# Four-layer graph network: single heads project values first, the adjacency is turned by DMA, wider ANDs, mask products summed in PSUM

## The chip, the cores and the metric

The kernel runs on one core of a Trainium2 chip. A core has four computing engines with queues of their own: TensorE (PE, matrix products into the PSUM banks), VectorE (DVE), ScalarE (ACT) and GpSimd (POOL), and a fifth, SyncE (SP), which here only issues DMAs; in the changed kernel POOL issues some too. The metric is the device time of one execution in microseconds (us), as the median of several runs.

## The reference

Sixteen graphs of 1024 nodes and 128 features go through four attention layers. In each one the layer's output is added to its input and normalized over the features:

```python
x = _layernorm(x + _L0_gnn_ref(x, adj, ...))   # typed attention
x = _layernorm(x + _L1_gnn_ref(x, adj, ...))   # single head, slope 0.01
x = _layernorm(x + _L2_gnn_ref(x, adj, ...))   # 8 heads, then a single head, with graph norms
x = _layernorm(x + _L3_gnn_ref(x, adj, ...))   # single head, slope 0.2
```

A single head computes `h = x @ W`, two scores per node `s = h @ a_src`, `t = h @ a_dst`, the weights `softmax(where(adj > 0, leaky_relu(s[:, None] + t[None, :]), -inf))`, and `weights @ h`. The eight-head part does this for eight heads of 16 features, with the features viewed as `(heads, nodes, 16)`. The typed layer 0 chooses one of eight bilinear scores by the entry of the adjacency. `adj` is an int32 array of 0 and 1, 4 MB a graph, with ones on the diagonal.

## The kernel before

The input of each graph is 1024 x 1024 adjacency entries and 1024 x 128 features; nodes lie as 128 partitions by G = 8 groups. All work of the fast path is written by `graph(b)` for b = 0 to 15 (L862), not issued at once: a `Recorder` (L113) collects the operations, and `rc.run` simulates engines with a cost for each operation and fixes one order per engine for all sixteen graphs together. Among operations that can start at the same time it takes the one with the lowest due time (`wanted`: its number in the program plus shifts from a table), lets up to two later graphs start ahead (`AHEAD`), and gives operations that ACT or DVE could do (`rc.either`: copies, scalings, biases, comparisons) to the one that is free earlier, with a handicap (`LATER`). All instructions of `graph` are issued from line L424, so rows of the profile are told apart by tiles. Each engine then runs its own list strictly in order. Tiles come from shelves with a fixed number of places: `maskT` 3, `row` 26 (4 KB a partition), `half` 11, `bank` 8 (the PSUM banks).

The steps of one graph:

- **Mask.** For each of eight row blocks SP loads 512 KB of int32 (`raw`), ACT casts it to bf16 (`eb`, a `half`), PE turns it in 128 x 128 squares, and ACT writes the squares to `maskT` as fp8, with value 2. Both ACT passes keep sums (`e_sum`, `e_sq`), by which an entry other than 0 and 1 is found at the end; then the general path runs instead.
- **Layer 0 (typed).** Two score products per square (128 x 512 columns, f32) are merged by DVE's COPY_PREDICATED on `maskT`; then a leaky relu, a maximum over the graph (`graph_max`), exponentials and the sum over the values.
- **Layers 1 and 3 (`single_head`, L798).** The weight of node j on all nodes is max(a_row, ratio_j) x mask, one DVE instruction for 128 x 1024 (`weights_of`). `a_row`, the factor of the receiving node repeated on all partitions, is made by `factors`: a matmul of a widened score vector (`srcw`) with hT in two halves of 512 columns, and two ACT exponentials of it. The scaled inputs are then the stationary operand and the weights move through in two halves of 512 columns (`av`), 32 passes of PE in all; the sums are copied to SBUF (`avT`) and only then multiplied with the layer's matrix (`w_v`).
- **Layer 2, eight heads.** exp(leaky_relu(s + t)) is split into two products by the sign of s + t. `mask_sums(g)` multiplies `maskT` with the low-slope factors of all heads (three bf16 parts each, `m4`): eight matmuls of 408 columns, and a DVE reduction of the three parts. `products(h)` makes, for two groups j at a time, the sign mask `q` (a `half`, fp8, ACT or DVE), ANDs it with `maskT` (DVE, 1024 uint16) and multiplies with 102 columns of `m4`. Its row of scores `s1_row` comes by DMA through DRAM (`s1d`).
- **Layer 2, second part (`projected_head`, L830).** Here the values are projected first and are the moving operand: 8 x 8 matmuls of 129 columns with squares of the weights as the stationary operand, and no product after it.

SP's queue, in a graph of the middle: the store of a finished graph, the eight adjacency loads and the load of the features of a coming one, the store `s1d`, and eight loads of `s1_row`.

Of the kernel before, what the change touches and what calls it, by code (L numbers as in the profile page):

```python
# [15 lines left out]
U8 = mybir.dt.uint8  # L16
AF = mybir.ActivationFunctionType
# [3 lines left out]
P = 128  # L21
D = 128
# [86 lines left out]
class Op:  # L109
    __slots__ = ("ways", "way", "skip", "graph", "rank", "before", "after", "ready", "slots", "missing", "late")  # L110


class Recorder:  # L113
# [4 lines left out]
    DMA_RATE, DMA_FIXED = 370.0, 2200.0  # L118

    def __init__(self, nc, tc):  # L120
        self.nc, self.tc, self.ops, self.graph = nc, tc, [], 0
        self.access = {}
        self.rate, self.used = [0.5], collections.Counter()
# [37 lines left out]
    def cost_of(self, engine, name, args, kw, outs, ins):  # L161
# [6 lines left out]
        if engine == "tensor":  # L168
            n = self.width(o)
            left = kw.get("lhsT", args[1] if len(args) > 1 else None)  # L170
            left = left.ap if isinstance(left, View) else left
            apart = abs(list(left.ap)[-1][0]) > 4
            if name == "transpose":
                return 112.0 if f32 else 62.0 if apart else 45.0, 165.0
            if f32:
                return 2 * max(n * 2 / 2.4, 238.0 if apart else 112.0), 165.0
            return max(n * 0.478 if n > 300 else n * 0.43, 45.0), 165.0
# [3 lines left out]
        if engine == "gpsimd":  # L181
            return 300.0, 50.0
# [32 lines left out]
    def either(self, *ways, skip=None):  # L215
# [4 lines left out]
        op.graph, op.ways, op.way, op.skip = self.graph, [], None, skip  # L220
# [39 lines left out]

    WINDOW, BUSY = 3413.0, 0.9

    def spend(self, t, work):

        while True:
            w = int(t // self.WINDOW)
            while len(self.rate) <= w:
                self.rate.append(1.0 if self.used[len(self.rate) - 1] > self.BUSY * self.WINDOW else 0.5)
            room = (w + 1) * self.WINDOW - t
            took = min(room, work / self.rate[w])  # L270
            self.used[w] += took
            t += took
            work -= took * self.rate[w]
            if work <= 1e-6:
                return t

    def run(self, rank, window, later):
# [62 lines left out]
        def admit(i):  # L340
            for way in ops[i].ways:
                pools[way[0]].append((i, way, ranks[i] + (later.get(way[0], 0) if len(ops[i].ways) > 1 else 0)))
# [25 lines left out]
        while len(order) < n:  # L368
# [38 lines left out]
            end = self.spend(t, way[4]) if way[0] == "tensor" else t + way[4]  # L407
# [28 lines left out]
def gnn_stack_kernel(ctx: ExitStack, tc: tile.TileContext, w: dict, out: bass.AP):  # L436
# [11 lines left out]
    def fast_path(stack):  # L448
# [144 lines left out]
        def row_weights(scores, name):  # L593
            src_wide = const([P, P], name + "_srcw")
            nc.vector.tensor_copy(src_wide, scores[0].to_broadcast([P, P]))
            return src_wide, scores[1]

        shift = const([P, P], "shift")
        nc.vector.memset(shift, 0.0)
        nc.vector.tensor_copy(shift[:, 0 : D - 1], ident[:, 1:D])
        nc.vector.memset(shift[0:1, 0 : D - 1], -1.0)

        def without_first(wt, name):
            ps = ps_const(D)
            nc.tensor.matmul(ps, lhsT=shift, rhs=wt, start=True, stop=True)
            t = const([P, D + 1], name)
            mean = ppool.tile([P, 1], F32, tag="mean", name="mean")  # L610
            nc.vector.tensor_reduce(mean, ps, AX.X, ALU.add)
            nc.vector.tensor_scalar(mean, mean, 1.0 / D, None, ALU.mult)
            nc.vector.tensor_scalar(t[:, 0:D], ps, mean, None, ALU.subtract)
            nc.vector.tensor_copy(t[:, D : D + 1], ident[:, D - 1 : D])
            return t

        w1_r, w2b_r, w3_r = row_weights(w1_s, "l1"), row_weights(w2b_s, "l2b"), row_weights(w3_s, "l3")
        w1_v, w3_v = without_first(w1, "w1_v"), without_first(w3T, "w3_v")
        w2b_e = const([P, D + 1], "w2b_e")
        nc.vector.tensor_copy(w2b_e[:, 0:D], w2b)  # L620
        nc.vector.tensor_copy(w2b_e[:, D : D + 1], w2b_s[1])
# [19 lines left out]
        e_sum = const([P, B, G], "e_sum")  # L641
        e_sq = const([P, B, G], "e_sq")
# [19 lines left out]
        PLACES = {"maskT": 3, "row": 26, "half": 11}  # L662
# [8 lines left out]
        shelves["dram"] = Shelf("dram", [dram.tile([NH, N], F32, tag=f"s1d{k}", name=f"s1d{k}")[:, :] for k in range(2)])  # L671

# [23 lines left out]
        def copy(dst, src):  # L696
            rc.either(("scalar", "copy", (dst, src), {}), ("vector", "tensor_copy", (dst, src), {}))

        def affine(dst, src, scale, shift):
# [3 lines left out]
                ("vector", "tensor_scalar", (dst, src, scale, shift, ALU.mult, ALU.add), {}),  # L703
            )

        def scaled(dst, src, scale):
# [3 lines left out]
                ("vector", "tensor_scalar", (dst, src, scale, None, ALU.mult), {}),  # L710
            )
# [48 lines left out]
        def graph_max(v):  # L760
# [4 lines left out]
            rc.tensor.transpose(ps[0:1, :], top, ident)  # L765
            top1 = small("top1", 1, 1)
            rc.vector.tensor_reduce(top1, ps[0:1, :], AX.X, ALU.max)
            ps = bank(1)
            rc.tensor.matmul(ps, lhsT=ones[0:1, :], rhs=top1, start=True, stop=True)
            return ps  # L770

        def factors(src_wide, hT, s2, alpha, e):
# [3 lines left out]


            c2 = small("c2", P, 2)
            rc.vector.tensor_scalar(c2, coef[alpha], graph_max(s2), None, ALU.mult)
            rc.scalar.activation(e, s2, AF.Exp, bias=c2[:, 0:1])  # L780
            ratio = small("ratio", P, G)
            rc.scalar.activation(ratio, s2, AF.Exp, bias=c2[:, 1:2], scale=alpha - 1.0)
            a_row = row(N)
            for k, c in enumerate(HALVES):
                ps = bank(H, P)
                rc.tensor.matmul(ps, lhsT=src_wide, rhs=hT[:, c, :], start=True, stop=True)
                rc.scalar.activation(
                    a_row[:, k * H * P : (k + 1) * H * P], ps.rearrange("p g q -> p (g q)"), AF.Exp,
                    bias=c2[:, 1:2], scale=1.0 - alpha,
                )  # L790
# [7 lines left out]
        def single_head(x, hT, maskT, weights, wv, alpha, e, rden, finish):  # L798

            src_wide, dst = weights  # L800
            s2_ps = bank(G)
            for j in range(G):
                rc.tensor.matmul(s2_ps[:, j : j + 1], lhsT=hT[:, j, :], rhs=dst, start=True, stop=True)
            s2 = small("s2c", P, G)
            rc.vector.tensor_copy(s2, s2_ps)
            a_row, ratio = factors(src_wide, hT, s2, alpha, e)
            xe = row(G, D)
            for j in range(G):
                scaled(xe[:, j, :], x[:, j, 1 : D + 1], e[:, j : j + 1])
            av = [bank(H, P) for _ in HALVES]  # L810
            for j in range(G):
                prob = weights_of(j, a_row, ratio, maskT)
                for k in range(2):
                    rc.tensor.matmul(
                        av[k], lhsT=xe[:, j, :],
                        rhs=prob[:, k * H * P : (k + 1) * H * P], start=(j == 0), stop=(j == G - 1),
                    )
            avT = row(G, P)
            for k, c in enumerate(HALVES):
                copy(avT[:, c], av[k])  # L820
            for g0 in range(0, G, 3):
                n = min(3, G - g0)
                o = bank(n, D + 1)
                for i in range(n):
                    rc.tensor.matmul(o[:, i, :], lhsT=avT[:, g0 + i, :], rhs=wv, start=True, stop=True)
                rc.vector.reciprocal(rden[:, g0 : g0 + n].unsqueeze(2), o[:, :, D : D + 1])
                for i in range(n):
                    finish(g0 + i, o[:, i, 0:D], rden[:, g0 + i : g0 + i + 1])

        def projected_head(hT, maskT, src_wide, w_e, alpha, e, rden, finish):  # L830

            s2 = small("s2c", P, G)
            val = row(G, D + 1)
            parts = []
            for g0 in range(0, G, 3):
                n = min(3, G - g0)
                ps = bank(n, D + 1)
# [3 lines left out]
                rc.vector.tensor_copy(s2[:, g0 : g0 + n].unsqueeze(2), ps[:, :, D : D + 1])  # L841
            a_row, ratio = factors(src_wide, hT, s2, alpha, e)
# [19 lines left out]
        def graph(b):  # L862
# [4 lines left out]
            for ib in range(G):  # L867
                raw = row(N, dt=I32)
                rc.sync.dma_start(out=raw, in_=adj_b[ib])
                eb = tile_on("half", [P, N], BF16)  # L870
                rc.scalar.activation(eb, raw, AF.Identity, accum_out=e_sum[:, b, ib : ib + 1])
                ps = bank(G, P, dt=BF16)
                for j in range(G):
                    rc.tensor.transpose(ps[:, j, :], eb.rearrange("p (q g) -> p g q", g=G)[:, j, :], ident_bf)
# [224 lines left out]
            for g in range(G):  # L1099
                mask_sums(g)  # L1100
# [745 lines left out]
```

## Time and profile before

| | before |
|---|---|
| median of 3 runs | 2647.28 us (2645.2 to 2647.3) |
| the profiled execution: span | 2644.0 us, 3.3 us under the median |
| PE busy | 2531.0 us (96%) |
| DVE busy | 2386.2 us (90%) |
| ACT busy | 2014.7 us (76%) |
| POOL busy | 12.7 us |
| moved by DMA | 156.39 MB, 59 GB/s over the span |
| mean granted TensorE clock | 0.985 |

The table shows one execution. The page gives each engine's busy time, and 40 slices of the span with a digit for the tenths of it that the engine was busy. Its groups give the count, the busy time, the mean duration in ns and the idle time before; its list of DMA issues gives the count, the size and the median us from issue to landing. The timeline lists runs of equal instructions with start, length and count. An f32 matmul shows as two passes of PE.

### The profile page before, as it was taken

The page shows a single profiled execution, that of the slowest core. Times are in us where ns is not written, and L with a number is a line of the kernel's source. Part 1 is how long each engine was busy: PE and PEld are TensorE (multiplying, and loading weights), DVE is VectorE, ACT ScalarE, POOL GpSimd, SP SyncE. Part 2 cuts the span into 40 slices and gives each one's busy share as a digit, 9 for nine tenths or more (in the row PEclk, how much of TensorE's full clock was granted, in tenths as well). Part 3 has the DMA queues.
Part 4 walks back from the last instruction along what each step waited for, and adds up shares of the span by engine and source line. Part 5 has one row for each costly group of instructions (what it writes and reads, how often), then busy time and mean ns, then how long its engine had stood idle before and what let it go on. Part 6 is the DMA issues. An engine that isn't in the chain of part 4 may idle for free.

```text
span 2644.0 us, 50556 instructions
## 1 busy us (share of the span) xinstructions
PE 2531.0 (96%) x19561; PEld 1789.1 (68%) x19561; DVE 2386.2 (90%) x5995; ACT 2014.7 (76%) x3598; POOL 12.7 (0%) x74
## 2 busy tenths in 40 slices
PE   6989999999999999999999999999999999999875
PEld 3657777667677676777767677766777776676753
DVE  4689999989899999999999899999999999899884
ACT  5666887978878697887969778797887878686851
POOL 0000000000000000000000000000000000000000
PEclk9999999999999999999999999999999999999887
DMA  6010112021210202121021212102121120210100
GB/s 238 1 65 1 65 64 81 1 81 65 81 65 16 105 27 81 65 81 65 1 91 55 81 65 81 65 1 80 65 81 65 58 87 1 81 65 9 65 9 10
DMA packets 75562, 156.39 MB, mean 59 GB/s; under 512 B 6705, under 2 KB 42417, under 8 KB 75313
## 3 DMA queue, kind: packets, MB, share of 16 engines
q1 hardware_dynamic: 75312, 153.07, 16.5%
q8 instruction: 156, 2.56, 0.4%
q14 instruction: 94, 0.76, 0.1%
HBM read 144.13 MB, written 8.91 MB: 58 GB/s over the span
## 4 chain that ended last, share of the span: by engine, by line
PE 86%; DVE 8%; DMA 3%; ACT 2%; issue 1%; SPq 0%; POOL 0%; DVEq 0%; ACTq 0%; POOLq 0%
PE bank L424 86%; DVE row L424 3%; DMA row<-in_adj_dram 2%; DVE half L424 1%; DVE x L424 1%; ACT half L424 1%; ACT row L424 1%; DMA row<-in_x_dram 0%; DVE mf L424 0%; DVE sums L424 0%; DVE bs L424 0%; DVE bank L424 0%; SPq L424 0%; DMA row<-s1d 0%; DMA l_as<-in_L_gnn_a_dram 0%
## 5 line engine op out<-in xcount | busy, mean ns | idle before, releaser
L424 PE MATMUL bank<-row,row 128*128 128x129 f32 (+1 forms) x6144 | 1431.2, 386 | 12.5 <-DVE row L424 5.2
L424 PEld LDWEIGHTS bank<-row,row 128*128 128x128 f32 x6144 | 835.1, 192 | 361.8 <-issue 302.6
L424 ACT ACTIVATE half<-row,bs2h 128x1024 fp8e4<-128x1024 f32 x799 | 859.7, 1141 | 8.7 <-PE bank L424 5.7
L424 PEld LDWEIGHTS <-half 128*128 128x128 fp8e4 (+1 forms) x9216 | 490.5, 103 | 155.5 <-issue 104.1
L424 DVE SCALAR_TENSOR_TENSOR row<-row,ratio,maskT 128x1024 f32<-128x1024 f32 x384 | 478.1, 1274 | 0.0
L424 PE MATMUL bank<-m,half 128*128 128x102 bf16 x8192 | 438.7, 208 | 5.7 <-DVE half L424 3.6
L424 DVE TENSOR_TENSOR half<-half,maskT 128x1024 uint16<-128x1024 uint16 x512 | 340.7, 680 | 0.4 <-ACT half L424 0.4
L424 ACT ACTIVATE row<-bank 128x512 f32<-128x512 f32 x256 | 151.4, 593 | 148.7 <-DVE bank L424 147.5
L424 PE MATMUL bank<-m,maskT 128*128 128x408 bf16 x1024 | 204.5, 357 | 1.1 <-DVE m L424 1.1
L424 DVE COPY_PREDICATED bank<-maskT,bank 128x512 f32<-128x512 uint8 x256 | 175.9, 692 | 25.5 <-PE bank L424 23.5
L424 DVE CUSTOM_DVE_ANT_0 row<-bank,row 128x512 f32<-128x512 f32 x256 | 172.2, 681 | 7.9 <-ACT row L424 7.6
L424 ACT ACTIVATE half<-row 128x1024 bf16<-128x1024 int32 x128 | 134.2, 1054 | 58.1 <-DMA row<-in_adj_dram 54.7
L424 DVE TENSOR_SCALAR half<-row,ns 128x1024 fp8e4<-128x1024 f32 x225 | 162.8, 748 | 1.1 <-PE bank L424 0.6
L424 PEld LDWEIGHTS <-maskT 128*128 128x128 fp8e4 x1024 | 98.4, 97 | 96.4 <-issue 5.1
L424 DVE TENSOR_REDUCE x<-bank 128x136 f32<-128x408 f32 x256 | 141.2, 575 | 10.4 <-PE bank L424 10.0
L424 ACT ACTIVATE row<-row,nm 128x1024 f32<-128x1024 f32 x128 | 136.5, 1136 | 0.5 <-DVE nm L424 0.4
L424 ACT ACTIVATE maskT<-bank 128x1024 fp8e4<-128x1024 bf16 x128 | 129.1, 1013 | 4.3 <-PE bank L424 3.9
L424 ACT COPY row<-bank 128x512 f32<-128x512 f32 x154 | 87.0, 581 | 54.8 <-PE bank L424 53.9
L424 PE MATMUL bank<-ident,row 128*128 128x128 f32 x640 | 103.7, 286 | 21.1 <-ACT row L424 16.6
L424 DVE SCALAR_TENSOR_TENSOR row<-bank,rdens,row 128x128 f32<-128x128 f32 x384 | 114.8, 344 | 1.2
L424 PEld LDWEIGHTS bank<-ident,row 128*128 128x128 f32 x640 | 80.4, 146 | 50.3 <-ACT row L424 23.5
L424 ACT ACTIVATE sq<-row 128x128 f32<-128x128 f32 x256 | 76.6, 300 | 41.9 <-DVE row L424 39.9
(223 smaller groups left out, 2693.2 us busy)
## 6 DMA issues: line engine op xcount, KB each, us to landing
row<-in_adj_dram SPq DMA_DIRECT2D x128, 512.0 KB, 8.6
row<-s1d SPq DMA_DIRECT2D x128, 512.0 KB, 8.3
row<-in_x_dram SPq DMA_DIRECT2D x16, 512.0 KB, 11.6
out_dram<-row SPq DMA_DIRECT2D x16, 512.0 KB, 4.0
a_raw<-in_L_gnn_a_dram SPq DMA_DIRECT2D x1, 512.0 KB, 5.5
s1d<-s1t SPq DMA_DIRECT2D x16, 32.0 KB, 1.8
w<-in_L_gnn_W_dram SPq DMA_DIRECT2D x2, 64.0 KB, 4.0
l_as<-in_L_gnn_a_dram SPq DMA_DIRECT2D x2, 64.0 KB, 4.2
```

The costliest lines, as they stand in the source:

```text
L424: done = getattr(getattr(self.nc, engine), name)(*[real(a) for a in args], **{k: real(a) for k, a in kw.items()})
```

## The change

- **Single heads.** `single_head` is gone; layers 1 and 3 use `projected_head` too. One product per group gives the values and both scores (130 columns: 128 values, and the two score vectors as further columns, made by `value_weights`). For layers 1 and 3 the weights have their mean over the outputs removed.
- **Row factor through DRAM.** `factors` computes the factor as 128 x 8 on ACT, turns it on PE, copies it (`aT`, DVE), stores 4 KB to DRAM (`a_d`) and loads it back with all 128 partitions reading the same row (512 KB), both on SP. Three times a graph.
- **Graph maximum.** One product turns and repeats the partial maxima; one DVE reduction over 128 columns finishes.
- **Adjacency.** Graph 0 goes the old way. For the other fifteen, POOL issues a DMA that casts the graph's int32 to bf16 in a DRAM buffer (`dram2`, two places), SP issues eight turning DMAs (1024 x 128 to a `half`) and eight stores to a second DRAM buffer (`dram3`), and POOL issues a DMA that loads it into `maskT` with a cast to fp8. The test for other entries becomes a tree of bitwise ORs on DVE. The mask's value is 1 instead of 2.
- **Wider ANDs.** The sign masks are made for four groups at a time, on the `row` shelf; one AND covers 2048 uint16.
- **Mask sums.** Up to three groups of receiving nodes share a PSUM bank, and the three bf16 parts are added by separate matmuls of 136 columns into the same place; a plain copy replaces the reduction.
- **Head values.** The multiplication of values by factors covers four heads in one instruction.
- **Order.** `row` has 30 places, `half` 3. The planner's costs, handicaps, shift table and per-graph shifts are other numbers, and the clock model of TensorE is left out of it, so all engines' orders differ throughout. In the new order SP's sixteen turning DMAs and stores of a graph lie between the store of a finished graph with the load of features, and the next head's `a_d`.

The core of the diff:

```diff
-    PLACES = {"maskT": 3, "row": 26, "half": 11}
+    PLACES = {"maskT": 3, "row": 30, "half": 3}
...
+            rc.tensor.matmul(ps, lhsT=top.to_broadcast([P, P]), rhs=ident, start=True, stop=True)
+            top_all = small("top_all", P, 1)
+            rc.vector.tensor_reduce(top_all, ps, AX.X, ALU.max, negate=negate)
+            return top_all
...
+            a = small("a", P, G)
+            rc.scalar.activation(a, s1, AF.Exp, bias=c2[:, 1:2], scale=1.0 - alpha)
+            ps = bank(P)
+            rc.tensor.transpose(ps[0:G, :], a, ident)
+            aT = small("aT", G, P)
+            rc.vector.tensor_copy(aT, ps[0:G, :])
+            a_d = tile_on("dram1", [1, N])
+            rc.sync.dma_start(out=a_d.rearrange("o (g p) -> (o g) p", g=G), in_=aT)
+            a_row = row(N)
+            rc.sync.dma_start(out=a_row, in_=a_d[0].partition_broadcast(P))
...
-            a_row = row(N)
-            for k, c in enumerate(HALVES):
-                ps = bank(H, P)
-                rc.tensor.matmul(ps, lhsT=src_wide, rhs=hT[:, c, :], start=True, stop=True)
-                rc.scalar.activation(
-                    a_row[:, k * H * P : (k + 1) * H * P], ps.rearrange("p g q -> p (g q)"), AF.Exp,
-                    bias=c2[:, 1:2], scale=1.0 - alpha,
-                )
...
+                scratch = tile_on("dram2", [N, N], BF16)
+                rc.gpsimd.dma_start(
+                    out=scratch.rearrange("(g p) m -> p g m", g=G), in_=adj[b].rearrange("(p g) m -> p g m", g=G)
+                )
+                upright = tile_on("dram3", [N, N], BF16)
+                for t in range(G):
+                    turned = tile_on("half", [P, N], BF16)
+                    rc.sync.dma_start_transpose(out=turned, in_=scratch[:, t * P : (t + 1) * P])
+                    rc.sync.dma_start(out=upright[t * P : (t + 1) * P, :], in_=turned)
+                rc.gpsimd.dma_start(out=maskT, in_=upright.rearrange("(p g) n -> p g n", g=G))
+                n = G * N // 4
+                seen = row(n, dt=U16)
+                flat = maskT.rearrange("p g n -> p (g n)").bitcast(U16)
+                rc.vector.tensor_tensor(seen, flat[:, 0:n], flat[:, n : 2 * n], ALU.bitwise_or)
+                while n > LEFT:
+                    n //= 2
+                    rc.vector.tensor_tensor(seen[:, 0:n], seen[:, 0:n], seen[:, n : 2 * n], ALU.bitwise_or)
+                rc.vector.tensor_tensor(bits, bits, seen[:, 0:LEFT], ALU.bitwise_or)
...
+            def mask_sums(g0):
+                n = min(3, G - g0)
+                ps = bank(n, NH, C1)
+                for i in range(n):
+                    g = g0 + i
+                    for j in range(G):
+                        for k in range(3):
+                            rc.tensor.matmul(
+                                ps[:, i], lhsT=maskT[:, j, g * P : (g + 1) * P], rhs=m4[:, :, j, k, C1:C2],
+                                start=(i == 0 and j == 0 and k == 0), stop=(i == n - 1 and j == G - 1 and k == 2),
+                            )
+                copy(mf[:, :, g0 : g0 + n, :], ps.rearrange("p g h c -> p h g c"))
...
-                for j in range(0, G, 2):
-                    q = tile_on("half", [P, 2, N], F8)
+                for j in range(0, G, H):
+                    q = row(H, N, dt=F8)
...
-            single_head(y1, hT, maskT, w1_r, w1_v, 0.01, exps[:, b, 0, :], rdens[:, b, 0, :], finish1)
+            projected_head(hT, maskT, w1_v, 0.01, exps[:, b, 0, :], rdens[:, b, 0, :], finish1)
...
-            single_head(y3, hT, maskT, w3_r, w3_v, 0.2, exps[:, b, 2, :], rdens[:, b, 2, :], finish3)
+            projected_head(hT, maskT, w3_v, 0.2, exps[:, b, 2, :], rdens[:, b, 2, :], finish3)
```

## Prediction

> **What bounds the kernel now.** I read the page's busy shares and its slices first: TensorE (PE) is at 9 in nearly every slice, VectorE (DVE) at 8 to 9.
>
> ```profile
> span 2644.0 us, 50556 instructions
> ...
> PE 2531.0 (96%) x19561; PEld 1789.1 (68%) x19561; DVE 2386.2 (90%) x5995; ACT 2014.7 (76%) x3598; POOL 12.7 (0%) x74
> ...
> PE   6989999999999999999999999999999999999875
> ...
> DVE  4689999989899999999999899999999999899884
> ```
>
> Then busy time by stretch (columns: stretch, its length, then PE, PEld, DVE, ACT, POOL, clock, DMA share, GB/s) and the waits of PE in the long middle stretch.
>
> ```profile
> 385.00:2420.00 2035.00, 2026.61 (x15879) 1434.53 (x15878) 1915.91 (x4808) 1640.02 (x2928) 7.25 (x49) 1.00 0.18 62
> 2420.00:2644.00 224.00, 160.74 (x1204) 118.52 (x1201) 168.84 (x403) 111.51 (x222) 0.39 (x2) 0.85 0.08 26
> ```
>
> ```profile
> PE bank L424 <- ACT half L424: 7.0, 7, 1.8
> ```
>
> In the 2035 us in the middle PE idles 8 us and its largest wait is 7 us: PE sets the pace. DVE is at 94%, so it stands next in line. The queue of SyncE (SP) gives the period: one graph's result is stored at 1010.81, the next one's at 1166.47, so a graph costs 155.7 us, and 2035 us are 13.1 periods. DVE is busy 0.941 of that, 146.6 us a graph; ACT 125 us.
>
> ```profile
> 1010.81 0.58 SPq L424 DMA_DIRECT2D out_dram<-row  x1
> ...
> 1166.47 0.58 SPq L424 DMA_DIRECT2D out_dram<-row  x1
> ```
>
> **TensorE, part by part.** A matmul's mean duration contains its pipeline, so I take paces from unbroken runs in the timeline (start, length, count of passes; an f32 matmul is two passes): (length less one mean duration of its group) over (count less one).
>
> ```profile
> 870.03 1.15 PE L424 MATMUL bank<-ident_bf,half 128*128 128x128 bf16 x16
> 917.65 4.85 PE L424 MATMUL bank<-row,row 128*128 128x129 f32 x42
> 933.50 10.56 PE L424 MATMUL bank<-m,maskT 128*128 128x408 bf16 x54
> 955.31 1.84 PE L424 MATMUL bank<-l_dst,row 128*128 128x1 f32 x16
> 971.06 3.98 PE L424 MATMUL bank<-m,half 128*128 128x102 bf16 x84
> 1145.63 9.67 PE L424 MATMUL bank<-row,row 128*128 128x512 f32 x22
> 1155.27 1.57 PE L424 MATMUL bank<-w_v,row 128*128 128x129 f32 x12
> ```
>
> So 512 columns cost 0.432 us a pass, 129 columns 0.111, the projection w_v 0.117, the one-column product 0.106, a bf16 turn 0.061, 408 columns 0.192, 102 columns 0.045. Per graph:
> - Gone: 64 turns of the adjacency, 3.9 us. Two single heads of the old form, each 32 passes of 512 (13.8), 16 one-column (1.7), 16 of w_v (1.9) and 4 of srcw at 512 columns (1.7): 38.2 together. The middle head's 4 row passes, 1.7. The mask sums' 64 x 0.192 = 12.3. Sum 56.1.
> - Come: two heads in the middle head's form, each 128 passes x 0.111 (14.2) and 16 x 0.117 (1.9): 32.2. Three turns of the factor (one f32 pass each) 0.4. Mask sums in 192 matmuls of 136 columns; the 102-column row reloads weights each time at 0.045, so by columns 0.060 and 11.5. Sum 44.1. The new maximum (one 128-column product for a turn and a broadcast) is even.
>
> PE needs 155.7 - 12.0 = 143.7 us a graph, if nothing makes it wait.
>
> **VectorE and ScalarE.** The instruction orders of the two builds give the counts for the whole kernel, these rows (count | busy, mean ns) the prices:
>
> ```profile
> L424 DVE TENSOR_TENSOR half<-half,maskT 128x1024 uint16<-128x1024 uint16 x512 | 340.7, 680 | 0.4 <-ACT half L424 0.4
> ...
> L424 ACT ACTIVATE half<-row 128x1024 bf16<-128x1024 int32 x128 | 134.2, 1054 | 58.1 <-DMA row<-in_adj_dram 54.7
> ...
> L424 ACT ACTIVATE maskT<-bank 128x1024 fp8e4<-128x1024 bf16 x128 | 129.1, 1013 | 4.3 <-PE bank L424 3.9
> ```
>
> Wider ANDs: 512 x 0.680 become 256 x 1.213 (0.52 ns an element and 0.15 fixed, worked out from that row and the 128-column ones): -38 us in the kernel. Mask-sum reductions gone (128 x 0.579): -74; fewer multiplies for the head values: -29. The planner also hands out the either-engine work anew: 51 more comparisons on DVE (0.748): +38; fewer PSUM copies and biases: -74; head values now read from PSUM: +50 against -34; other scalings +15. New: the OR tree, 15 graphs x 2.87 = +43; two-column score copies and factor copies +21; mask-sum copies +8; the rest about +4. Sum -70 us over 16 graphs. About 25 fewer instructions a graph also means less overlap of neighbours (some 0.07 us each), so I take -2 us: DVE needs 144.6 a graph. **DVE is now as tight as PE.** ACT loses 120 casts and 120 mask writes (2.3 us a pair, 1.25 + 1.21 with their accumulator reads), 96 exponentials of the row and more: 390 us, down to about 101 a graph; it bounds nothing.
>
> **The factor's trip through DRAM.** Three times a graph aT goes out and a row comes back; DVE's weights wait for it. The chain of waits holds the same two steps for s1d:
>
> ```profile
> 162.97 1.84 DMA s1d<-s1t
> 164.94 5.19 DMA row<-s1d
> ```
>
> So 7.2 us. By the new order DVE has 6.4, 5.5 to 6.4 and 9 to 9.6 us of other work between aT and the first weight (summing rows). Waits of 0.8, 1.3 and nothing, some 2 us a graph. DVE at 144.6 + 2, with 2 to 3 us for two engines that wait on each other (in 315 to 385 us, at its best, DVE reaches 97%): **149.5 us a graph**, 6.2 less. Over 13.1 periods: -81 us.
>
> **The adjacency by DMA.** Each graph from the second on gets one cast by POOL's queue (4 MB to 2 MB, DRAM to DRAM), then on SP eight turning DMAs and eight stores in waves of 3, 3 and 2 (three `half` places), then a load with cast by POOL. No engine waits for these directly. But SP's queue is in order: the 16 DMAs stand behind the result's store and **in front of the next head's factor store**. By the new order DVE has 26 us of work between the last scaling of the result and that aT. A wave ends 1.8 + 3t + 0.5 us after it starts (1.8 from the small store, 0.5 an issue, t the pace of a turning DMA); all three: 6.9 + 8t. For t:
>
> ```profile
> row<-in_adj_dram SPq DMA_DIRECT2D x128, 512.0 KB, 8.6
> ...
> out_dram<-row SPq DMA_DIRECT2D x16, 512.0 KB, 4.0
> ```
>
> The result's store is 1024 pieces of 512 B in 4.0 us; a turning DMA reads 1024 pieces of 256 B. Less 1.8 fixed: t = 2.2 us, and 24.5 us in all. The Trainium skill ("DMA: Bandwidth & Descriptors", Latency and other measured facts) has 261 GB/s for such a transpose with strided rows; estimated from it, 256 KB take 1.0 us, and the burst 15. No run here shows a transpose; I take the row, the slower one. Both fit into 26 us, the row barely: cost nothing, and 8 us a graph for each further microsecond of t. The mask is wanted after 51 us of DVE work: 24.5 + 2.5 for the last store + 8 for the load (2 MB at the adjacency's pace, eight of them within 5.4 + 8.6 us, 300 GB/s) leave 16 us of cover.
>
> One rule speaks against POOL's queue: "SBUF — State Buffer", SBUF: two separate sides, says that DMAs issued there starve while DVE runs a two-port instruction, with an example five times as long. At five times the load would take 40 us, overrun its cover by 16 us and cost that each period. But by the rows the candidates (comparisons at 0.748 and small SBUF scalings) are some 10% of DVE's time, so I take 10 us instead of 8, and nothing on the path. This trace has no POOL DMA to show either.
>
> **Start and end.** Before, DVE begins graph 1's masked selects at 107.9 us. Now they stand behind graph 0's eight weights of its first head, hence its trip: some 20 us later, with half of PE's time filled: +10; and that factor store stands behind 15 turning DMAs and the second cast. At 30 us a cast (6 MB at 300 GB/s is 20; half that pace is 40) they end near 104, before it is wanted; at 40 they are late by some 6. I take +15, ends 5 and 40. At the end three trips lie bare, 7.2 against 2.3 for the old row, less the work saved: +4.
>
> Sum against the profiled execution: 2644 - 81 + 15 + 4 = 2582; its median stands 3.3 us higher: **2585 us**. Measurement can tell 0.2%, 5 us.
>
> **Rivals.**
> - *The turning burst blocks SP* (ends slower). For it: 1024 small pieces each, beside POOL's cast on the same DMA engines, and the burst fits with 2 us to spare. Against: SP mostly idles now. From t = 3.2 the 6.2 us gain is gone (6.9 + 25.6 - 26 = 6.5); at t = 5 a graph stalls 21 us: 2585 + 13.1 x 21 = 2860. I give it 28%, from 2660 up.
> - *PE stays the only bound* (DVE's waits hide): 144.5 a graph, 2644 - 147 + 19 + 3 = 2519. Against it: DVE's 144.6. 10%.
> - *The gains are used up* by longer trips among crowded DMAs (5 us a graph more): 2585 + 13.1 x 5 = 2650. 10%, spread over 2635 to 2660.
> - The likeliest: 52%, its own range 2545 to 2635.
>
> **How the numbers follow.** Faster: 52 + 10 and a little of the third, 0.63; same 0.05; slower 28 and the rest, 0.32. The range 2510 to 2720 leaves out few of the fast cases and about half of the blocked ones.
>
> **What would show it.** Right: PE's row,row passes of 512 columns halve to 1024 (the typed layer's own), period near 149.5 between result stores, DVE and PE both at 96 to 98% in the middle, DVE's longest wait one for the row from a_d, 1 to 2 us each. Wrong: SP waiting long on `half` or `up`, a_d stores issued long after aT, DVE waiting for maskT, or turning DMAs landing after more than 8 us each.

## The result, and the profile after

The changed kernel takes 2667.6 us (median of 4 runs, 2656.67 to 2669.51) against 2647.03 us: ratio 1.007, interval 1.0048 to 1.0092. It is slower by 0.7%, where 2585 us and a gain of 2.4% had been forecast. Its profiled execution is the fastest of the four (2656.67 us), 11 us under the median: its span is 2654.7 us, 10.7 us above the 2644.0 of before. All figures from the profile below belong to this execution.

First the page of the changed kernel: its span, the busy times, two rows of the 40 slices, and the chain that ended last, by engine.

```profile
span 2654.7 us, 56604 instructions
...
PE 2390.6 (90%) x22981; PEld 2029.6 (76%) x22981; DVE 2326.3 (88%) x5599; ACT 1683.7 (63%) x3029; POOL 43.9 (2%) x104
...
PE   3999999999989999899998999999999999998865
...
DVE  2689899988989999899988989999998998999884
...
PE 43%; DVE 40%; DMA 12%; issue 3%; ACT 2%; SPq 0%; ACTq 0%; DVEq 0%; POOL 0%; POOLq 0%
```

PE lost 140 us of busy time and became idle for a little more (2654.7 - 2390.6 = 264 us against 113). The chain shows what took PE's place. In the same chain before, PE had 86% and DMA 3%; now DVE has 40% and DMA 12%:

```profile
PE 86%; DVE 8%; DMA 3%; ACT 2%; issue 1%; SPq 0%; POOL 0%; DVEq 0%; ACTq 0%; POOLq 0%
```

Then the stretch from 385 to 2420 us (columns: stretch, length, PE, PEld, DVE, ACT, POOL, clock, DMA share, GB/s).

```profile
385.00:2420.00 2035.00, 1910.41 (x18538) 1620.31 (x18536) 1861.93 (x4474) 1360.69 (x2446) 31.65 (x76) 0.98 0.35 89
```

The waits of DVE and of PE in that stretch (us in total, times, longest):

```profile
DVE row L412 <- DMA row<-a_d: 61.9, 23, 6.2
DVE row L412 <- ACT row L412: 51.9, 92, 2.4
DVE rdens L412 <- PE bank L412: 26.4, 21, 2.6
...
PE bank L412 <- DVE row L412: 81.3, 59, 5.7
PE bank L412 <- DVE m L412: 22.1, 12, 2.3
```

Before, PE's largest wait there was 7.0 us. Now it waits 81.3 us for rows of weights from DVE, and DVE waits 61.9 us for the row factor that comes back from DRAM.

The sixteen stores of results tell where the 10.7 us lie. The first is issued at 383.37 before and 361.09 after; thirteen graphs later it is 2418.04 and 2397.63. So the steady period is 156.51 us before and 156.66 after: **the 6.2 us a graph were not gained at all**. The start is 22.3 us shorter and the stretch from the fourteenth store to the end of the span 31.1 us longer (257.1 against 226.0): 13 x 0.15 - 22.3 + 31.1 = 10.8.

### The profile page after: what moved, and what is told of

The parts are those of the page before. It is cut to its first block, busy times and chain, and to the rows that moved or that the text cites. A ratio compares the mean times of both kernels' runs of the same rounds, so it can differ in the third digit from the quotient of the medians.

```text
span 2654.7 us, 56604 instructions
## 1 busy us (share of the span) xinstructions
PE 2390.6 (90%) x22981; PEld 2029.6 (76%) x22981; DVE 2326.3 (88%) x5599; ACT 1683.7 (63%) x3029; POOL 43.9 (2%) x104
## 4 chain that ended last, share of the span: by engine, by line
PE 43%; DVE 40%; DMA 12%; issue 3%; ACT 2%; SPq 0%; ACTq 0%; DVEq 0%; POOL 0%; POOLq 0%
PE bank L412 42%; DVE row L412 25%; DMA row<-a_d 7%; DVE x L412 5%; DMA a_d<-aT 3%; ACT row L412 2%; DVE bank L412 2%; DVE bs L412 1%; DMA row<-in_x_dram 1%; DVE sums L412 1%; DVE m L412 1%; DVE rs_q L412 1%; DVE mf L412 1%; DMA row<-s1d 1%; DVE rdens L412 0%
## 5 line engine op out<-in xcount | busy, mean ns | idle before, releaser
L412 PEld LDWEIGHTS bank<-row,row 128*128 128x128 f32 x9216 | 1144.9, 197 | 333.7 <-issue 248.3
L412 ACT ACTIVATE row<-row,bs2h 128x1024 fp8e4<-128x1024 f32 x748 | 797.7, 1141 | 20.4 <-DMA row<-s1d 14.3
L412 PE MATMUL bank<-m,row 128*128 128x102 bf16 x8192 | 404.1, 208 | 5.1 <-DVE m L412 4.6
L412 PEld LDWEIGHTS <-row 128*128 128x128 fp8e4 x8192 | 392.9, 97 | 7.9 <-issue 4.8
L412 DVE TENSOR_TENSOR row<-row,maskT 128x2048 uint16<-128x2048 uint16 x256 | 306.5, 1213 | 7.6 <-ACT row L412 7.5
L412 PE MATMUL bank<-m,maskT 128*128 128x136 bf16 x3072 | 219.5, 231 | 34.0 <-DVE m L412 31.1
L412 PEld LDWEIGHTS <-maskT 128*128 128x128 fp8e4 x3072 | 209.4, 100 | 50.9 <-issue 36.3
L412 DVE TENSOR_SCALAR row<-row,ns 128x1024 fp8e4<-128x1024 f32 x276 | 198.0, 744 | 0.0
L412 DVE COPY_PREDICATED bank<-maskT,bank 128x512 f32<-128x512 uint8 x256 | 173.6, 686 | 10.9 <-PE bank L412 10.2
L412 ACT ACTIVATE row<-row,top_all 128x1024 f32<-128x1024 f32 x128 | 137.7, 1139 | 1.9 <-DVE top_all L412 1.9
L412 ACT ACTIVATE row<-row,gb,ga 128x128 f32<-128x128 f32 (+1 forms) x64 | 39.2, 661 | 99.7 <-DVE gb L412 99.7
## 6 DMA issues: line engine op xcount, KB each, us to landing
adj<-in_adj_dram POOLq DMA_DIRECT2D x15, 2048.0 KB, 17.6
```

Source lines behind the costliest of these rows:

```text
L412: done = getattr(getattr(self.nc, engine), name)(*[real(a) for a in args], **{k: real(a) for k, a in kw.items()})
```

## The experiments

The times of each row are medians; ratios are to the kernel before, run beside it. Where an expectation names theories by letters, they hold for the runs sent together: e1 to e4, e5 to e8 (A and B are other theories there), e9 to e12.

In e1 to e5 and e7 to e9 an operation is exchanged or left out only when it is issued, after the orders of all engines have been fixed, so every engine's list stays that of the changed kernel. The cuts show what is issued in the end, not the lines that do the exchange. In those that leave work out (e1, e2, e3, e7, e8, e9) the threshold of the final test is raised, so that the general path never runs.

### e1, e2, e3: without the trips, without the turning, without both

```diff
 e1: the factor's store is left out, the row load reads a fixed row of the features
-            rc.sync.dma_start(out=a_row, in_=a_d[0].partition_broadcast(P))
+            rc.sync.dma_start(out=a_row, in_=some)
 e2: cast to DRAM, turning DMAs and their stores are left out; maskT is loaded from the adjacency itself
-                rc.gpsimd.dma_start(out=maskT, in_=upright.rearrange("(p g) n -> p g n", g=G))
+                rc.gpsimd.dma_start(out=maskT, in_=adj[b].rearrange("(p g) n -> p g n", g=G))
 e3: both
```

> The changed kernel with every engine's order kept, but the factor's trip taken away: the 48 stores of aT to a_d are left out and the row load reads a fixed row of the input instead (so the factors are other numbers). It no longer waits for aT, only for its place. Theory A (the trip through DRAM is what eats the gain: DVE waited 78 us for row<-a_d, PE waited with it, and PE's clock fell in those gaps): 2560 to 2590 us. Theory B (the sixteen turning DMAs and stores in front of it on SP are the cause): little change, 2640 to 2670, since the row load still stands behind them. Theory C (DVE and PE are equally tight and wait on each other everywhere): 2620 to 2650.

> The changed kernel with every engine's order kept, but the adjacency chain cut short: POOL's cast to DRAM, the 120 turning DMAs and their 120 stores are left out, and POOL loads maskT straight from the int32 adjacency with a cast (so the mask is not turned). Theory B (the burst on SP delays the factor, or its traffic slows the trip): 2570 to 2600 us. Theory A (the trip itself, and the loads of s1_row in front of it): 2645 to 2665, a few us less at the start. Theory C: 2650 to 2665.

> Both cuts of the two other kernels together, every engine's order kept: no trip and no turning DMAs. Theory A: within 10 us of the kernel without the trip alone. Theory B: within 10 us of the one without the turning alone. Theory C: 2610 to 2650, no better than its better half by more than 10 us. If both causes count, it is lower than either by 20 us or more.

| run | time us | ratio (interval) | period | DVE's wait for the row, 385 to 2420 us |
|---|---|---|---|---|
| changed | 2667.6 | 1.0070 (1.0048 to 1.0092) | 156.66 | 61.9 |
| e1, no trip | 2577.5 | 0.9745 (0.9729 to 0.9762) | 151.58 | none |
| e2, no turning | 2591.6 | 0.9797 (0.9781 to 0.9814) | 152.00 | 7.6 |
| e3, neither | 2564.0 | 0.9689 (0.9673 to 0.9705) | 151.34 | none |

In the period e1 brings 5.1 us a graph, e2 4.7 and both together 5.3; in the whole time 90, 76 and 104 us, not 166. Each alone brings nearly all of what both bring in the middle, so it is one cause that needs both. e1 and e2 came within a range that had been expected, of theory A and of theory B. e3 fits none: it lies 13 us under e1, where A said 10 at most and two separate causes 20 at least. In e2 the 48 trips are all made, and yet DVE hardly waits for them. **The trip costs something only when the turning of the adjacency is there, and the turning costs something mostly through the trip.** What of the turning meets the trip was open.

### e4 and e5: the trips on another queue

```diff
-            rc.sync.dma_start(out=flat, in_=aT)          # and the row load
+            rc.scalar.dma_start(out=flat, in_=aT)        # e4; rc.gpsimd in e5
```

> The changed kernel with every engine's order kept, but the 48 stores a_d and 48 row loads are issued by ACT at the same place in the order instead of SP, so that they do not stand in SP's queue behind the eight s1_row loads. In the trace one a_d store took 7.4 us to land behind 4 MB of s1_row loads. Theory A in the form 'the trip is long because it queues behind other DMAs of its own queue': the wait of DVE for row<-a_d falls from 78 us to under 30 and the time to 2600 to 2630, unless ACT, which now stands still for each trip, delays the sign masks. If the trip is long whatever the queue: 2655 to 2700.

> All 48 factor trips (4 KB store and 512 KB row load) issued by POOL's queue instead of SP's; every engine's order of instructions as in the changed kernel. Theory A (the small store is late because it lands behind the 4 MB of eight row loads of s1d on SP's own queue): the delay from store to row load of every third trip falls from 4.7 us in the mean to below 2, and the time to 2610 to 2640. Theory B (the DMA engines themselves are full at these places, whatever the queue): the delays stay, as they did when ACT issued them, and the time stays at 2655 to 2690.

Measured: 2668.7 us by ACT (ratio 1.0086, 1.0061 to 1.0111), as expected for a trip that is long whatever the queue, and 2701.1 by POOL (1.0214, 1.0197 to 1.0231), slower than either theory had said. SP's queue is not the cause: by ACT the wait for the row stays at 64.3 us. The waits of POOL in e5 show where its trips lose time (start, length, instruction, and in brackets the idle time before it and what ended it):

```profile
1113.11 0.51 POOL L416 DMA_DIRECT2D a_d<-aT  x1 [42.66 <-DVE row L416]
1113.62 0.72 POOL L416 COPY row<-exps 128x8 f32<-128x8 f32 x1
1118.12 0.53 POOL L416 DMA_DIRECT2D row<-a_d  x1 [3.78 <-DMA a_d<-aT]
1118.64 0.90 POOL L416 DMA_DIRECT2D adj<-in_adj_dram  x1
...
1184.75 0.54 POOL L416 DMA_DIRECT2D maskT<-up  x1 [40.95 <-DMA up<-half]
1185.29 0.51 POOL L416 DMA_DIRECT2D a_d<-aT  x1
1185.80 0.21 POOL L416 COPY row<-exps 128x8 f32<-128x8 f32 x1
1194.08 0.55 POOL L416 DMA_DIRECT2D row<-a_d  x1 [8.07 <-DMA a_d<-aT]
```

A store of 4 KB takes over 4 us while only SP's eight loads of `s1_row` are ahead of it, on another queue, and 8.8 us behind the load of `maskT`; alone it takes 1.2 (at 2575.16, below). POOL's list is in order, so here the cast of the next graph can start only after the third head's row load. So e5 already tells the two large DMAs apart. From the end of the copy of `aT` to the first weights the third trip takes 9.4 us in the mean (12.1 in the changed kernel) and the first, behind the load of `maskT`, 13.4 (9.0). The latter fits e5's longer time. e4 is a weaker test: in ACT's list the row load stands behind other work, at 1098.12 to 1103.89 us behind four exponentials and two copies, so a late issue is part of its delay.

### e6: the s1 rows behind the trip

```diff
+            for j in rows[self.KEEP :]:        # six of the eight loads row<-s1d ahead of a trip
...
+                put.setdefault(trip, []).append(j)   # are issued behind its row load
```

> Only SP's order changes: of the eight row loads of s1d ahead of every third trip, the last six go behind the trip; nothing is left out. Theories A and B both have the trip behind two loads (1 MB) that have landed by then: its delay falls from 4.7 to about 1.3 us, DVE's waits for the row by up to 3.4 us a graph, so 2667 - 13 x 3.4 = 2623, 2615 to 2640. If the comparisons then wait for the later s1 rows, or if the wait only moves to another place because DVE and PE hold each other up there anyway: 2650 to 2680.

Measured: 2660.9 us, ratio 1.0059 (1.0042 to 1.0076); the gain of 7 us lies within the intervals, in the range given for a wait that only moves. The delay from store to row load of the third trip fell from a mean of 4.7 us to 2.9, but DVE's waits only from 61.9 to 58.6. So the s1 rows ahead of the trip are not what makes the row late. They still share the DMA engines with it in this run; e12 leaves them in their place, and the waits go.

### e7, e8, e9: less work for DVE, for PE, for both

```diff
 e7: the AND with maskT becomes an AND with a constant
-   rc.vector.tensor_tensor(bits_q, bits_q, maskT[:, j : j + H, :].bitcast(U16), ALU.bitwise_and)
+   rc.vector.tensor_scalar(bits_q, bits_q, 0x3838, None, ALU.bitwise_and)
 e8: of the mask sums' three products per square only k = 0 is made
+                            if k > 0 and not (i == n - 1 and j == G - 1 and k == 2):
+                                product.swap = "leave out"
 e9: both
```

> The AND of each sign mask with the adjacency (256 x 1.213 us) becomes an AND of the sign mask with a constant: the adjacency is left out of the low-slope selection, all else stays, PE's work too. If it takes half as long, DVE is lighter by 9 us a graph. Theory C (DVE and PE are tied: each waits for the other, some 9 us a graph without the trips): less than half of the 9 x 15 = 135 us is gained, 2600 to 2650, with PE's waits nearly all that is left. Theory D (DVE alone sets the pace, its waits are the trips'): 2530 to 2570.

> Of the mask sums' three products per square (192 of 136 columns a graph) only the first is made: 128 x 0.060 = 7.7 us a graph less for PE; the sums lack the two lower parts of each value. DVE's work stays. Theory C (tied): 30 to 60 us of the 115 are gained, 2605 to 2640. Theory D (DVE alone sets the pace): under 20 us, 2650 to 2670. If PE alone set the pace: 2555.

> Both lightenings at once: the ANDs of the sign masks with a constant instead of the adjacency (DVE 8.5 us a graph less), and one of three products per square in the mask sums (PE 7.7 us a graph less). Alone they gained 9 and 8 us of the 2667.6. Theory C (each hides the other, stage by stage): together they gain clearly more than the 17 us of the sum, 40 to 110, so 2560 to 2630. Theory E (the DRAM trips and what crowds them set the pace through the waits, which neither lightening shortens): the sum again, 2640 to 2660.

| run | time us | ratio (interval) | period |
|---|---|---|---|
| e7, DVE lighter | 2658.3 | 1.0049 (1.0028 to 1.0071) | 157.43 |
| e8, PE lighter | 2659.5 | 1.0066 (1.0041 to 1.0090) | 156.31 |
| e9, both | 2613.8 | 0.9871 (0.9853 to 0.9888) | 153.48 |

Between the first result and the fourteenth, DVE's busy time fell by 7.6 us a graph in e7 and PE's by 5.5 in e8, less than the 7.7 of the matmuls left out, at a granted clock of 0.96 in place of 0.98. Yet neither engine alone is worth anything that the intervals can tell. e7 came out as neither theory had said; e8 fell into the range of theory D (DVE alone sets the pace), which e7 contradicts. Together the two are worth 54 us (1.0070 to 0.9871), three times the sum, as theory C had said of e9. The time saved turned into waits. From 385 to 2420 us DVE in e7 works 107 us less and waits 78 us more for PE and 20 more for rows from ACT. PE in e8 works 67 us less and waits 84 us more for DVE's `row` and `top`. In single stretches the two engines take turns as the bound. In one stretch of 7.7 us (columns as above) of the changed kernel, and the same stage of e7:

```profile
993.46:1001.16 7.70, 7.70 (x153) 7.69 (x152) 7.70 (x24) 7.63 (x10) 0.00 (x0) 1.00 0.81 210
...
1047.36:1055.06 7.70, 5.78 (x33) 3.86 (x32) 7.70 (x15) 2.34 (x7) 0.00 (x0) 1.00 0.09 34
```

```profile
993.32:1001.02 7.70, 7.70 (x148) 7.69 (x146) 7.00 (x24) 7.70 (x10) 0.00 (x0) 1.00 0.79 204
...
1047.22:1054.92 7.70, 5.77 (x32) 3.80 (x31) 7.70 (x16) 2.36 (x8) 0.00 (x0) 1.00 0.10 37
```

With the ANDs (first row of each) PE is full before and after, and a lighter DVE only idles there; with a head's weights and the typed layer's selects (second row) DVE is full and PE idles. No average of the two shows this.

### e10, e11, e12: POOL's two large DMAs held back

What starts beside the late trips gave the last theory. These are the instructions of POOL, SP and DVE in the changed kernel around a third trip:

```profile
1087.90 0.20 POOL L412 COPY row<-exps 128x8 f32<-128x8 f32 x1 [44.77 <-ACT exps L412]
1088.14 0.89 POOL L412 DMA_DIRECT2D adj<-in_adj_dram  x1
...
1080.11 4.84 SPq L412 DMA_DIRECT2D row<-s1d  x8
1089.57 0.29 SPq L412 DMA_DIRECT2D a_d<-aT  x1
1097.03 0.34 SPq L412 DMA_DIRECT2D row<-a_d  x1
...
1104.37 8.46 DVE L412 SCALAR_TENSOR_TENSOR row<-row,ratio,maskT 128x1024 f32<-128x1024 f32 x7 [5.41 <-DMA row<-a_d]
```

The chain of the changed kernel has the times from issue to landing (start, length): of this trip, of the row load of the next first trip, and of a trip at the end, with little else moving:

```profile
1089.57 7.31 DMA a_d<-aT
1097.03 7.23 DMA row<-a_d
...
1169.30 9.13 DMA row<-a_d
...
2575.16 1.20 DMA a_d<-aT
2576.42 3.70 DMA row<-a_d
```

and these are the stretches of 4 us from there:

```profile
1088.00:1092.00 4.00, 3.52 (x11) 1.49 (x10) 3.50 (x8) 3.13 (x7) 0.99 (x2) 1.00 1.02 419
1092.00:1096.00 4.00, 4.00 (x37) 4.00 (x37) 4.00 (x6) 4.00 (x7) 0.00 (x0) 1.00 1.12 244
1096.00:1100.00 4.00, 4.00 (x45) 3.99 (x44) 2.96 (x7) 4.00 (x5) 0.00 (x0) 1.00 1.12 212
1100.00:1104.00 4.00, 0.46 (x8) 0.27 (x5) 0.00 (x0) 4.00 (x5) 0.00 (x0) 1.00 1.03 254
1104.00:1108.00 4.00, 2.20 (x10) 2.23 (x11) 3.63 (x4) 4.00 (x5) 0.00 (x0) 0.68 0.07 15
```

In POOL's list the cast of the next graph's adjacency (6 MB moved) stands right behind the copy of `e` into the values of the third head. That copy runs 1.7 us before the same head's `aT` is stored. So the DMA engines are full (share over 1) for the length of the trip, DVE stands still from 1099 to 1104, and PE stands nearly still from 1100 to 1104. The cast itself is wanted only by the turning DMAs at 1141. Likewise POOL issues the load of `maskT` just behind the start of the first head's trip:

```profile
1168.03 0.29 SPq L412 DMA_DIRECT2D a_d<-aT  x1
1168.38 0.54 POOL L412 DMA_DIRECT2D maskT<-up  x1 [41.76 <-DMA up<-half]
```

e10 and e11 hold one of the two back, e12 both:

```diff
+            if i in behind:   # i: the cast (e10, e12) or the load of maskT (e11, e12)
+                read = self.nc.gpsimd.tensor_copy(self.spare, real(behind[i])[:, 0:8])
```

`behind[i]` is the first row of weights that the trip beside it makes. POOL's list is in order, so this small read keeps the DMA behind it until that row exists. The load of `maskT` also goes behind POOL's copy for that head. Nothing is left out.

> One wait more, nothing left out: POOL reads 8 columns of the first weights of the third head before it issues the next graph's cast, so the cast (6 MB) starts when that trip has landed instead of 1 us before its store. Theory F (the trips are late because POOL's two large DMAs of a graph start within a microsecond of two of the three trips): the third trip falls from 10 to 16 us to 9.3, the length of the work that covers it, DVE's waits for it vanish (2.3 to 6 us a graph), 2667 - 13 x 3.3 = 2624, 2610 to 2640. If the eight row loads of s1d alone delay it: 2655 to 2670.

> Likewise the load of maskT waits for the first weights of the head whose trip it stood beside, and starts some 10 us later; nothing is left out. Theory F: the first trip falls from 8.5 to 10.5 us to 7, DVE's waits there (0.5 to 3 us a graph) vanish: 2667 - 13 x 1.7 = 2645, 2635 to 2655. If the mask is then late for its first use: 2670 or more.

> Cast and load of maskT both held back in this way. Theory F: nearly all that leaving the turning out gained (2591.6): 2595 to 2620, faster than the kernel before. If each only moves its collision to other DMAs: 2640 to 2670.

Measured, with the mean time from the end of the copy of `aT` to the start of the first weights, over 13 graphs of the middle (the work of DVE in between covers 7 us in the first head and 9 in the third):

| run | time us | ratio (interval) | period | first trip | third trip | DVE's wait for the row |
|---|---|---|---|---|---|---|
| changed | 2667.6 | 1.0070 (1.0048 to 1.0092) | 156.66 | 9.0 | 12.1 | 61.9 |
| e10, cast later | 2616.7 | 0.9892 (0.9869 to 0.9916) | 153.42 | 9.1 | 9.0 | 24.4 |
| e11, load later | 2634.3 | 0.9952 (0.9938 to 0.9966) | 154.96 | 7.3 | 12.1 | 42.4 |
| e12, both later | 2586.4 | 0.9777 (0.9761 to 0.9793) | 151.35 | 7.2 | 9.1 | 1.7 |

Each puts right the trip that it was aimed at and leaves the other as it was, and the gains add up: 51 + 33 = 84 against 81 together. e10 came within its expectation, e11 and e12 came out 1 and 9 us better than theirs. **e12 computes everything and is faster than both kernels**, 2.2% below the one before, 3.0% below the changed one. The page of e12:

```profile
span 2582.2 us, 56657 instructions
...
PE 2371.6 (92%) x22981; PEld 2013.4 (78%) x22981; DVE 2323.5 (90%) x5599; ACT 1681.8 (65%) x3029; POOL 85.8 (3%) x131
...
PE 48%; DVE 43%; ACT 3%; DMA 3%; issue 3%; SPq 0%; ACTq 0%; POOL 0%; POOLq 0%; DVEq 0%
```

DMA is back at 3% of the chain. A third trip of e12 with its cast, POOL first, then SP, then DVE:

```profile
916.84 0.44 POOL L448 COPY row<-exps 128x8 f32<-128x8 f32 x1 [44.79 <-ACT exps L448]
928.10 1.18 POOL L439 COPY spare<-row 128x8 f32<-128x8 f32 x1 [10.81 <-DVE row L448]
929.22 0.89 POOL L448 DMA_DIRECT2D adj<-in_adj_dram  x1
...
917.76 0.29 SPq L448 DMA_DIRECT2D a_d<-aT  x1
922.00 0.34 SPq L448 DMA_DIRECT2D row<-a_d  x1
...
926.76 6.06 DVE L448 SCALAR_TENSOR_TENSOR row<-row,ratio,maskT 128x1024 f32<-128x1024 f32 x5
```

The store still takes 4.2 us behind the s1 rows, and in the mean of the third trips the delay from store to row load is 4.1 us against 4.7 in the changed kernel. So what the cast lengthens is above all the row load. The weights start with no wait before them; and the cast, 11 us later than its queue would have started it, is done long before the turning begins at 963.82.

## Why the prediction was wrong, point by point

| step | predicted | changed | e12 |
|---|---|---|---|
| DVE's work a graph | 144.6 | 143.3 | 143.1 |
| its waits for the trips | 2 | 4.8 | 0.1 |
| its other idle time | 2.9 | 8.6 | 8.1 |
| period | 149.5 | 156.66 | 151.35 |
| in the middle | -81 | +2 | -67 |
| start | +15 | -22 | -26 |
| end | +4 | +31 | +32 |

(DVE's work: busy time from the first result's store to the fourteenth, divided by 13; the waits as listed above, divided by 13. The middle is 13 periods against before's, whose mean is 156.51 us. The prediction took 155.7 from one pair of stores.)

- **The work was priced nearly right.** DVE came out 1.3 us below its sum. PE's busy time between the same stores is 147.0 us a graph in the changed kernel and 145.7 in e12 (granted clock 0.98 and 0.99), against 143.7. The wide AND took 1213 ns, as worked out. ACT lost 331 us in the whole kernel, not 390.
- **The step that failed first is the factor's trip**, "waits of 0.8, 1.3 and nothing, some 2 us a graph". The 7.2 us came from the first s1 trip, with little else moving. Bare, at the end of the changed kernel, a trip is shorter: 1.20 us for the store and 3.70 for the row in the chain at 2575.16. In the middle, where the row load is on the chain beside POOL's cast or its load of `maskT`, that load alone takes 6.7 to 9.8 us in 18 of 23 trips (in four of the other five the store was the long one), and a store up to 8.5. From the copy of `aT` to the first weights pass 9 to 16 us in the third head and 7 to 11 in the first. The waits stood where none was expected, in the third head (3.0 us a graph), and 1.7 in the first; the second head, expected to wait, never did. They cost somewhat more than their length: with 60 us of them gone in the middle, e12's middle is 69 us shorter (13 x 5.31) and its span 72.5.
- **Behind it is the sentence on the adjacency that "no engine waits for these directly".** True, but they take the DMA engines. I followed SP's order in detail and asked of POOL's DMAs only whether they would be done in time, never when they start. POOL's list, with the cast right behind the third head's copy of `e`, could have been read beforehand. The rival "the gains are used up by longer trips among crowded DMAs" names the right mechanism; it had 10%.
- **The second failed step is "2 to 3 us for two engines that wait on each other".** DVE is idle for some 8 us a graph even when trips and turning are away: in e3 its work is 143.1 of 151.34, and in e12, with the waits for the trips gone, 8.1 are left. I had taken DVE's best 70 us as a measure. But the windows shown of before had DVE idle for 2035 - 1915.9 = 119 us, 9.1 a graph, and I took all of it for slack under PE's bound. e7 to e9 show the mutual hold: of two engines with nearly equal sums, neither alone is the bound. But not all of the 8.1 us is PE's. DVE's longest list of waits in e12, from 385 to 2420 us, is for ACT:

```profile
DVE row L448 <- ACT row L448: 45.4, 90, 1.2
DVE rdens L448 <- PE bank L448: 35.8, 24, 3.1
```

  That is some 3 us a graph in short waits of half a microsecond, for an engine of which the prediction said that it bounds nothing. Its sum does not (104.5 us a graph), but DVE and ACT hand work to each other within a stage. What shorter waits for ACT would bring was not tried.
- **Start and end.** +15 and +4 were predicted, -22 and +31 came; in sum +19 and +9. DVE is busy 267.6 us ahead of the first result against 300.2 before, and 195.2 after the fourteenth against 169.2: so it seems that the new order does less for later graphs ahead of the first result, and has it to do at the end. e12 has nearly the same ends, so POOL's two DMAs are not behind them. Of the end's 31 us the bare trips take 6: without them (e1) it is 251.3 us long instead of 257.1. What the order costs in itself was not tried.
- **The turning burst, the rival with 28%, did not happen.** It was sized at 24.5 us and fits. At 1141.08 SP issues the first turning DMA, at 1164.5 the last store is out, and `aT` comes only at 1168.03. Over twelve graphs the burst took 21.2 to 25.1 us, and in eleven of them SP issued the store of `aT` within 0.03 us of the copy; in one it was 1.4 us late. Eight turning DMAs hold SP for 6.06 + 5.38 + 2.50 us, 1.7 each:

```profile
1141.08 6.06 SPq L412 DMA_TRANSPOSE half<-adj  x3
...
1149.83 5.38 SPq L412 DMA_TRANSPOSE half<-adj  x3
...
1159.60 2.50 SPq L412 DMA_TRANSPOSE half<-adj  x2
```

  Of the two paces weighed, t = 2.2 from the result's store (24.5 us in all) and 1.0, estimated from the Trainium skill ("DMA: Bandwidth & Descriptors", Latency and other measured facts; 15 us in all), the row was the nearer.
- **The rule of the Trainium skill on starved POOL DMAs** ("SBUF — State Buffer", SBUF: two separate sides) was kept small, and nothing here contradicts that: the load of `maskT` took 8.7 us in the median, 7.8 to 10.2. No run tests the rule, for in the 9 us beside such a load DVE ran hardly any of the candidates that the prediction names (no comparison, 0.2 us of SBUF scalings in the mean). What the load did to others was the point, not what others did to it.

That the forecast of 2585 us equals e12's 2586 is luck: there the middle gains 14 us less than predicted, and the ends cost 14 less.

## What to carry to other kernels

Follow every queue that issues DMAs to the moment at which a large transfer can *start*, not only to when it is wanted: in an in-order queue an operation with nothing to wait for runs as soon as the one ahead of it is done, whatever the plan had in mind, and a short trip beside it waits for its megabytes (here a row load of 512 KB took mostly 7 to 10 us in place of 3.7). A small read that holds such a transfer back until the trip has landed was worth 3% here. Where two engines have nearly equal sums, price the time that they hold each other up from the idle time that the second one shows over the whole steady stretch, not from its best moment.

## What was not expected of the hardware

- A store of 4 KB took 1.2 us from issue to landing with the DMA engines free. When other transfers of several MB were under way, up to 8.6 us passed from the store to the row load that waits for it, on ACT's and POOL's queues as well (e4 up to 6.1, e5 8.8 in the lines shown). How the DMA engines share themselves among queues was not examined.
- The cast of 4 MB to 2 MB from DRAM to DRAM landed in 17.6 us (median) beside the trips and s1 rows, and in 14.1 us when held back (e12): waiting 11 us, it was done only 8 later.
- After PE's pause at 1100 to 1104 the granted clock of the next 4 us was 0.68 (shown above). For the same 22981 matmuls PE is busy 2390.6 us in the changed kernel (mean clock 0.965) and 2371.6 in e12 (0.972), which pauses less: here the waits also cost 19 us of slower matmuls.
- An AND of 2048 uint16 with a constant took 682 ns (e7), with a second tensor 1213.
